# A hybrid layer in one launch: where the recurrence's first block of inputs is loaded, and where its batch statistics are put together

## The chip, the cores and the metric

The kernel runs on one core of one Trainium2 chip. The metric is the device time of one launch in microseconds (us), the median over several executions. A core has five engines that run their own instruction streams: TensorE (PE, matrix products), VectorE (DVE), ScalarE (ACT), GpSimd (POOL) and SyncE (SP). Transfers between the chip's memory and the on-chip memory (SBUF) are issued by SP here, except for those that add to what stands at their destination, which POOL issues. All of them are carried by the core's 16 DMA engines.

## The reference, cut to what matters

Everything is float32. An image is 64 x 64 cells with 128 features, and there are 16 of them. Layer 0 adds a grid recurrence (a two-dimensional LSTM) to its input. Layer 1 first adds a landmark attention over the 4096 tokens of each image, then the part that the change touches:

```
# t: 16 images x 4096 tokens x 128 features, after the attention
Wx   = einsum('bti,hi->bth', layernorm(t), W)
mean, var = over all 16*4096 tokens, for each of the 128 features
Wx   = (Wx - mean) * rsqrt(var + 1e-5) * gamma + beta
y_t  = sigmoid(Wx_t + y_{t-1} @ V.T)        # scan over the tokens of an image, y_{-1} = 0
out  = t + y
```

The normalisation needs `mean` and `var` of all tokens before the first sigmoid can be taken.

## The kernel before, in words

Five stages follow each other: group statistics of the input (to about 110 us), the grid LSTM (to about 1,430 us), the landmarks, the attention (up to 3,712 us) and the recurrence (to the end). The change touches the last two.

**The attention** (`attention`) walks over 128 groups of 512 tokens, eight (`Q`) to an image, in software-pipelined steps: `step(s)` for `s` from 0 to 144. In one step one group is projected (`new`, group s), one is weighed (`mid`, s-8), one is compared (`nxt`, s-15), one is attended (`cur`, s-16) and one is finished (`prev`, s-17). So the last sixteen steps project nothing new, and the very last finishes group 127. The order of the instructions on PE, DVE, ACT and POOL is the order in which the program is written (`tc.manual_schedule`); only SP's order is chosen by a scheduler. Values of an image, spread by heads, stand in `vs[b % 2]`, two buffers `at_vh0` and `at_vh1` of 16 KB per partition each; the even images use the first. Their last readers are the convolution over the tokens (`convolve`, line 1026, and `convolve_edges`, line 1038). For image 14 these are in steps 128 to 131.

Finishing a group means: `measure` (DVE, lines 1143 and 1144, then POOL, lines 30, 31, 1148 and 1149) and `normalise` (ACT, line 1154) make the layer norm, `turn_output` transposes it (PE, line 895), and `feed` multiplies it with W (PE, line 1161), takes the group's batch statistics into one entry of six numbers of `wx_stats` (DVE, line 1162), copies the product (ACT, line 1164) and stores it to `wx` in memory (SP, line 1165). `compare` makes DVE read four banks (line 1073, `topmost`). `output` makes `at_u`, the new t, on DVE (line 1135), and stores it to `t2` and `out` (SP, line 1137).

**The recurrence** (`recurrence`) doesn't scan 4096 tokens in order. An image is cut into 128 pieces of 32 tokens (`L = STEPS = 32`), which run side by side. Each piece begins 12 tokens (`WARM`) before its start to let the state converge, so a group of two images (`GI`) takes 12 + 32 = 44 rounds, plus one for a check whether the warm start agrees with the piece before. (If it doesn't, `in_order` does it again, token by token.) Eight such groups, `g` 0 to 7, run in four lanes: group g starts in round 0, 9, 18, 27, 45, 54, 63 and 72 (`starts`). The inputs of a group are loaded in two halves of 2.1 MB each, in four transfers a half: `w[1]` holds tokens 16 to 31 of each piece and is read in rounds 0 to 11 (the warm part) and 28 to 43 of the group, `w[0]` holds tokens 0 to 15 and is read in rounds 12 to 27. The tiles of the first kind have five buffers in turn, those of the second three. `due` says at which round a load stands in the program: `w[1]` ten rounds ahead of the group's start. A load whose buffer isn't free waits in SP's queue, and everything behind it waits too.

A round of one live group is a product with V (PE, line 1360), a scaled sum (DVE, line 1373) and a sigmoid (ACT, line 1381). The first round of a group has no product, and ACT reads the loaded input directly (line 1371), with the scale and shift that follow from the batch statistics (lines 1313 to 1317: DVE, POOL, DVE). Every second round of a group transposes two finished tokens (PE, line 1350) and copies them to `rc_tt` (ACT, line 1351, eight buffers); every fourth round POOL issues a transfer of 512 KB that adds `rc_tt` to `out` (line 1354). In a round the live groups follow each other on every engine in the order of their numbers, the copies come last.

The buffers of the loads, and their count, in the code before:

```
if n == 0:
    gr.w[h] = wp.tile([P, GI, G, HALF, C], F32, tag=f"w{h}", name=f"rc_w{h}", bufs=(3, 5)[h])
```

Of the kernel before, what the change touches and what calls it, by code (L numbers as in the profile page):

```python
# [8 lines left out]
F32 = mybir.dt.float32  # L9
AF = mybir.ActivationFunctionType  # L10
ALU = mybir.AluOpType
# [4 lines left out]
P = 128  # L16
# [3 lines left out]
HALF = STEPS // 2  # L20

AHEAD = 7
EPS = 1e-5


def inv_std(nc, pool, out, var, mhalf, tag):

    p, n = var.shape
    ve = pool.tile([P, n], F32, tag=f"{tag}_ve", name=f"{tag}_ve")
    nc.gpsimd.tensor_scalar(ve[:p], var, EPS, None, ALU.add)  # L30
    nc.gpsimd.tensor_tensor(out, ve[:p], mhalf[:p, :n], ALU.pow)


def group_stats(nc, tc, x, ident, mhalf, gmean, grstd, aside):
# [8 lines left out]
    with ExitStack() as ctx:  # L43
# [33 lines left out]
        def spread(v, copy):  # L77
# [3 lines left out]
            copy(ve, vg)  # L81
            nc.gpsimd.tensor_scalar(ve, ve, EPS, None, ALU.add)
            nc.gpsimd.tensor_tensor(grstd[:, v.cols], ve, mhalf[:, : v.n], ALU.pow)
# [61 lines left out]
def lstm_grid(nc, tc, x, fixed, stats, ident, mhalf, gmean, grstd, t1, acc):  # L145
# [17 lines left out]
    with ExitStack() as ctx:  # L163
# [110 lines left out]
        def factors(v):  # L274
# [4 lines left out]
            ve = sm.tile([P, 2, KT], F32, tag="ve", name="ls_ve")  # L279
            nc.gpsimd.tensor_scalar(ve[:, 0, :k], var, EPS, None, ALU.add)  # L280
            nc.gpsimd.tensor_scalar(ve[:, 1, :k], var, 1.0 + EPS, EPS * EPS, ALU.mult, ALU.add)
            nc.gpsimd.tensor_tensor(  # L282
# [145 lines left out]
def landmarks(nc, tc, acc, gamma, beta, wqkv, mask, ident, qm, km, pinvT):  # L428
# [12 lines left out]
    ITERS = 6  # L441
    GI = 8
    NT = NP * B // GI
    FLIP = range(NT * 3 // 8)
    W = GI // 2
    E = P // NP
# [348 lines left out]
    return a  # L795


def attention(nc, tc, t1, gamma, beta, wqkv, ident, mhalf, fixed, xp, rows, qm, km, pinvT, t2, wx, wx_stats, out):

# [5 lines left out]
    B, N, _ = t1.shape  # L807
    F = P
    M = km.shape[3]
    H = fixed[0].shape[1]  # L810
    DH = F // H
    K = N // P
    C = 4
    Q = K // C
    NP = H // 2
    E = W2 = 2 * DH
    GC = C * P
    BF = mybir.dt.bfloat16
    with ExitStack() as ctx:
        vp = ctx.enter_context(tc.tile_pool(name="at_v", bufs=1))  # L820
# [9 lines left out]
            return [bank(k, [P, GC]) for k in ks]  # L830

        bands, edges, wo, bo, wfT, ones, ones_b, minus, ident_b, heads, split, tops, avs = fixed
        vs = [vp.tile([P, H, K, DH], F32, name=f"at_vh{k}") for k in range(2)]
        R = vp.tile([P, K, H, DH], F32, name="at_R")

        low, high = slice(0, P // 2), slice(P // 2, P)
# [423 lines left out]
        with tc.manual_schedule(  # L1260
            engines={mybir.EngineType.PE, mybir.EngineType.DVE, mybir.EngineType.Activation, mybir.EngineType.Pool}
        ):
            projected(images[0])
            for g, a in enumerate(rows):
                group(g).xh = a
            turn_rows(group(0))
            for s in range(Q * (B + 2) + 1):
                step(s)


def recurrence(nc, tc, wx, wx_stats, t2, ffn_v, gamma, beta, ident, mhalf, out):

# [3 lines left out]
    B, H = wx.shape[:2]  # L1278
    N = t2.shape[1]
    L = STEPS  # L1280
    CH = N // L
    C = 16
    G = CH // C
    S = 4
    NB = L // S
    GI = 2
    LANES = 4
    PARTS = 8
    WARM = 12
    AGREE = 2.0 ** -18  # L1290
    NG = B // GI
# [2 lines left out]
    with ExitStack() as ctx:  # L1294
# [5 lines left out]
        with ExitStack() as fast:  # L1300
            wp = fast.enter_context(tc.tile_pool(name="rc_wp", bufs=1))
# [7 lines left out]
            vp = ps_t.tile([P, 4, P], F32, tag="t", name="rc_t")  # L1309
            nc.tensor.transpose(vp[:, 0, :], v, ident)  # L1310
            nc.vector.tensor_copy(vT, vp[:, 0, :])
            mv = cp.tile([P, 2], F32, name="rc_mv")
            nc.vector.bn_aggr(mv, wx_stats.rearrange("p c s -> p (c s)"))
            inv_std(nc, cp, scale, mv[:, 1:2], mhalf, "rc")
            nc.vector.tensor_mul(scale, scale, gamma)
            nc.vector.tensor_mul(shift, mv[:, 0:1], scale)
# [12 lines left out]

            def load(gr, n):  # L1330

                h, n = 1 - n // (PARTS // 2), n % (PARTS // 2)
                if n == 0:
                    gr.w[h] = wp.tile([P, GI, G, HALF, C], F32, tag=f"w{h}", name=f"rc_w{h}", bufs=(3, 5)[h])
                i, k = divmod(n, PARTS // 2 // GI)
                g = slice(k * G // 2, (k + 1) * G // 2)
                nc.sync.dma_start(
                    out=gr.w[h][:, i, g].rearrange("p g l c -> p (g l c)"),
                    in_=wx[gr.g * GI + i, :, h, g, :].rearrange("p g x -> p (g x)"),
                )  # L1340

            def turn(gr, s):

# [18 lines left out]
            def state(gr, n):  # L1362


                s = (n - WARM) % L
                w = gr.w[s // HALF][:, :, :, s % HALF, :]
                y = yp_.tile([P, GI, CH], F32, tag="y", name="rc_y", bufs=24)
                yg = y.rearrange("p i (g c) -> p i g c", c=C)
                gr.last = y
                if gr.z is None:  # L1370
                    nc.scalar.activation(yg, w, AF.Sigmoid, bias=shift, scale=scale)
                    return
                nc.vector.scalar_tensor_tensor(  # L1373
                    yg, w, scale, gr.z.rearrange("p i (g c) -> p i g c", c=C), ALU.mult, ALU.add
                )
                if n == WARM - 1:
                    gr.last = gr.y0 = yp_.tile([P, GI, CH], F32, tag="y0", name="rc_y0", bufs=LANES)
                    nc.vector.memset(gr.y0[:, :, 0:1], 0.0)
                    nc.scalar.activation(gr.y0[:, :, 1:CH], y[:, :, 0 : CH - 1], AF.Sigmoid, bias=shift)
                    return  # L1380
                nc.scalar.activation(y, y, AF.Sigmoid, bias=shift)  # L1381
                gr.ys[n - WARM] = y
# [10 lines left out]
            with tc.manual_schedule(  # L1393
                engines={mybir.EngineType.PE, mybir.EngineType.DVE, mybir.EngineType.Activation, mybir.EngineType.Pool}
            ):
                for t in range(max(starts) + ALL + 1):
# [10 lines left out]
                    for gr, n in live:  # L1407
                        s = n - WARM
# [75 lines left out]
@with_exitstack  # L1484
def kernel(ctx: ExitStack, tc: tile.TileContext, ins: dict, out: bass.AP):
    nc = tc.nc
    x = ins["x"]
    B, D0, D1, F = x.shape
    N = D0 * D1
    HEADS = ins["L1_attn_conv_w"].shape[0]  # L1490
    const = ctx.enter_context(tc.tile_pool(name="const", bufs=1))
    dram = ctx.enter_context(tc.tile_pool(name="scratch", bufs=1, space=DRAM))

    ident = const.tile([P, P], F32, name="ident")
    make_identity(nc, ident)
    mhalf = const.tile([P, 32], F32, name="mhalf")
    nc.gpsimd.memset(mhalf, -0.5)
    mask = head_mask(nc, const, HEADS)
    wqkv = const.tile([P, 3 * P], F32, name="wqkv")
    nc.scalar.dma_start(out=wqkv, in_=ins["L1_attn_w_qkv"])  # L1500
    gamma, beta, fgamma, fbeta = (
        column(nc, const, ins[f"L1_{k}"], k) for k in ("attn_gamma", "attn_beta", "ffn_gamma", "ffn_beta")
    )

    t1 = dram.tile([B, N, 2 * F + 4], F32, name="t1")
    t2 = dram.tile([B, N, F], F32, name="t2")
    wx = dram.tile([B, P, 2, N // 512, 256], F32, name="wx")
    pinvT = dram.tile([B, P, HEADS // 2 * D0], F32, name="pinvT")
    wx_stats = const.tile([P, B * N // 512, 6], F32, name="wx_stats")

    with tc.tile_pool(name="at_c", bufs=1) as ac, tc.tile_pool(name="at_x", bufs=1) as xp, tc.tile_pool(
        name="lmk", bufs=1
    ) as lmk:
        qm = lmk.tile([P, B, 2, D0], F32, name="qm")
        km = lmk.tile([P, B, 2, D0], F32, name="km")
        with tc.tile_pool(name="first", bufs=1) as first:
            acc = first.tile([P, 2, D0 * B // 2 // P, F], F32, name="acc")
            gmean = first.tile([P, B], F32, name="gmean")
            grstd = first.tile([P, B], F32, name="grstd")
            lw = [[ins[f"L0_conv_{k}{g}"] for g in GATES] for k in "wub"]  # L1520
            with tc.tile_pool(name="ls_c", bufs=1) as lc:
                start = ExitStack()
                cs = start.enter_context(tc.tile_pool(name="cb_s", bufs=1))
                cps = start.enter_context(tc.tile_pool(name="cb_ps", bufs=2, space=PSUM))
                fixed, jobs = attention_tiles(
                    nc, ac, cs, cps, dram, (N, F), ins["L1_attn_conv_w"], ins["L1_attn_w_out"],
                    ins["L1_attn_b_out"], ins["L1_ffn_W"], ident,
                )
                nc.vector.memset(acc, 0.0)
                lstm_fixed = lstm_tiles(nc, lc, (B, D0, F), *lw)  # L1530

                def stats(loads):
                    with start:
                        group_stats(nc, tc, x, ident, mhalf, gmean, grstd, jobs[:1] + loads + jobs[1:])

                lstm_grid(nc, tc, x, lstm_fixed, stats, ident, mhalf, gmean, grstd, t1, acc)
            rows = [load_rows(nc, xp, t1, 0, g) for g in range(3)]
            landmarks(nc, tc, acc, gamma, beta, wqkv, mask, ident, qm, km, pinvT)
        attention(
            nc, tc, t1, gamma, beta, wqkv, ident, mhalf, fixed, xp, rows, qm, km, pinvT, t2, wx, wx_stats,  # L1540
            out.rearrange("b i j f -> b (i j) f"),
        )
    recurrence(
        nc, tc, wx, wx_stats, t2, ins["L1_ffn_V"], fgamma, fbeta, ident, mhalf, out.rearrange("b i j f -> b (i j) f")
    )


# [19 lines left out]
```

## Time and profile before

| | |
|---|---|
| median of 3 runs | 4001.95 us (3993.2 to 4007.41) |
| the profiled execution, its own time | 4002.48 us |
| its span, first to last instruction | 4000.7 us |
| PE, DVE, POOL, ACT busy, share of the span | 94%, 77%, 71%, 63% |
| attention's last matrix product with W ends | 3711.9 us |
| first sigmoid of the recurrence starts | 3724.0 us |
| first sigmoid of groups 1, 2, 3 | 3745.5, 3764.0, 3780.8 us |
| first sigmoid of groups 4, 5, 6, 7 | 3823.1, 3847.1, 3874.3, 3895.3 us |
| last sigmoid | 3986.4 us |
| share of the DMA engines busy, 3,712 to 4,001 us | 97% |

The profile comes from one execution. Its page has the busy time of each engine, the span in 40 slices, the DMA queues, the chain of work that ended last, and groups of like instructions with the idle time ahead of them and what ended it. Closer views are answers to questions on the trace: the instructions in order of time ("start us, us, engine line op out<-in xcount [idle before <-releaser]"), the DMA traffic of a stretch, and the busy time of each engine in a stretch, with the clock that TensorE was granted (1.00 is full speed). Queue q1 carries what SP issues, queue q0 what POOL issues.

### The profile page before, as it was taken

The numbers are of one execution on the slowest core, as the hardware profiler recorded it, in microseconds if no ns is written. First come the engines' busy times: TensorE is split into PE (matmuls) and PEld (weight loads), VectorE is DVE, ScalarE is ACT, GpSimd is POOL, SyncE is SP. The second block draws the span as 40 slices with busy tenths as digits, with TensorE's granted clock in tenths as the row PEclk, the third lists the DMA queues.
The fourth block names the chain that finished last, engine by engine and source line by source line (L and its number), as shares of the span: only waits on it lengthen the run. The fifth ranks groups of instructions, "written<-read, shape, count | busy, mean of one in ns | idle before, by whom it ended". The sixth has DMA issues, their size and how long they took to land. (4 is left out here: it accounts for less than half of the span.)

```text
span 4000.7 us, 98082 instructions
## 1 busy us (share of the span) xinstructions
PE 3759.9 (94%) x36706; PEld 2534.3 (63%) x36706; DVE 3074.8 (77%) x7378; ACT 2510.8 (63%) x5131; POOL 2833.5 (71%) x4111
## 2 busy tenths in 40 slices
PE   6899999999999979789999999999999999988697
PEld 5667655555676669556666666666666666654486
DVE  8699999988898864338788788878887878757465
ACT  0466566566676644346777777777677777645597
POOL 0577877778888844158888888888888888876133
PEclk9899999999999979899999999999999999989798
DMA  9123332333332200113333333333333333223799
GB/s 339 59 73 81 82 83 81 84 83 86 87 87 79 72 26 5 45 26 85 89 92 87 95 89 88 95 84 96 85 92 95 83 95 85 82 65 91 243 267 175
DMA packets 500464, 383.75 MB, mean 96 GB/s; under 512 B 35976, under 2 KB 466960, under 8 KB 499984
## 3 DMA queue, kind: packets, MB, share of 16 engines
q1 hardware_dynamic: 477354, 340.74, 29.7%
q0 software_dynamic: 17728, 34.61, 4.8%
q8 instruction: 292, 4.78, 0.5%
q10 hardware_dynamic: 4902, 2.08, 0.2%
q14 instruction: 188, 1.54, 0.1%
HBM read 172.82 MB, written 204.48 MB: 94 GB/s over the span
## 5 line engine op out<-in xcount | busy, mean ns | idle before, releaser
L1018 POOL TENSOR_TENSOR at_total<-at_total,at_e 128x512 f32<-128x512 f32 x480 | 611.5, 1274 | 117.5 <-ACT at_e L991 86.2
L254 ACT ACTIVATE ls_g<-ls_z,ls_b 128x304 f32<-128x304 f32 (+26 forms) x950 | 496.3, 545 | 231.8 <-PE ls_z L252 197.4
L247 PE MATMUL ls_z<-ls_xn,ls_w 128*128 128x432 f32 (+28 forms) x1700 | 591.3, 495 | 3.9 <-POOL ls_xn L239 3.6
L247 PEld LDWEIGHTS ls_z<-ls_xn,ls_w 128*128 128x128 f32 x1700 | 312.8, 193 | 193.0 <-issue 98.4
L885 POOL TENSOR_SCALAR at_T<-at_T,at_nb 128x128 f32<-128x128 f32 x512 | 403.8, 797 | 13.3
L954 DVE TENSOR_REDUCE at_mxq<-at_bank 128x1 f32<-128x512 f32 x512 | 327.8, 683 | 83.4 <-PE at_bank L951 83.2
L252 PE MATMUL ls_z<-ls_hsum,ls_u 128*128 128x304 f32 (+26 forms) x1140 | 373.8, 465 | 0.0
L991 ACT ACTIVATE at_e<-at_bank 128x512 f32<-128x512 f32 x512 | 264.3, 603 | 116.3 <-PE at_bank L985 115.6
L1073 DVE TENSOR_REDUCE at_cmx<-at_bank 128x8 f32<-128x512 f32 x512 | 317.5, 683 | 18.2 <-PE at_bank L1066 12.5
L282 POOL TENSOR_TENSOR ls_tt<-ls_ve,mhalf 128x8 f32<-128x8 f32 (+2 forms) x190 | 314.2, 1654 | 15.8
L1102 ACT ACTIVATE at_eT<-at_bank 128x512 f32<-128x512 f32 x512 | 264.3, 603 | 75.0 <-PE at_bank L1099 74.8
L252 PEld LDWEIGHTS ls_z<-ls_hsum,ls_u 128*128 128x128 f32 x1140 | 215.9, 198 | 128.6 <-issue 78.0
L252 PE MATMUL ls_z<-ls_h,ls_u 128*128 128x304 f32 (+26 forms) x760 | 261.4, 468 | 27.1 <-DVE ls_h L369 27.1
L361 POOL TENSOR_TENSOR ls_g<-ls_g,ls_cell 128x304 f32<-128x304 f32 (+26 forms) x190 | 179.2, 943 | 127.5 <-ACT ls_g L254 111.3
L299 ACT ACTIVATE ls_tt<-ls_tt,ls_nb 128x128 f32<-128x128 f32 (+9 forms) x632 | 261.1, 479 | 4.3 <-POOL ls_nb L294 4.3
L365 ACT ACTIVATE ls_g<-ls_cell 128x304 f32<-128x304 f32 (+26 forms) x190 | 93.2, 491 | 263.3 <-DVE ls_cell L364 258.4
L239 POOL TENSOR_TENSOR ls_xn<-ls_xn,grstd 128x304 f32<-128x304 f32 (+26 forms) x190 | 202.8, 1068 | 51.1 <-DVE ls_xn L236 48.8
L1373 DVE SCALAR_TENSOR_TENSOR rc_y<-rc_w,rc_scale,rc_z 128x256 f32<-128x256 f32 x344 | 155.5, 480 | 107.1 <-PE rc_z L1360 105.4
L1360 PE MATMUL rc_z<-rc_y,rc_vT 128*128 128x256 f32 x688 | 186.1, 408 | 39.2 <-ACT rc_y L1381 28.4
L252 PEld LDWEIGHTS ls_z<-ls_h,ls_u 128*128 128x128 f32 x760 | 144.0, 198 | 120.8 <-issue 53.1
L1154 ACT ACTIVATE at_z<-at_u,at_nb,at_r 128x128 f32<-128x128 f32 x512 | 211.6, 505 | 11.9 <-POOL at_nb L1149 11.9
L1164 ACT COPY at_fx<-at_bank 128x512 f32<-128x512 f32 x128 | 133.0, 1039 | 126.2 <-DVE wx_stats L1162 103.5
(261 smaller groups left out, 9429.6 us busy)
## 6 DMA issues: line engine op xcount, KB each, us to landing
t<-ls_tt SPq DMA_DIRECT2D x392, 130.0 KB
at_T<-t SPq DMA_DIRECT2D x128, 264.0 KB
gs_xb<-in_x_dram SPq DMA_DIRECT2D x64, 512.0 KB
at_xh<-t SPq DMA_DIRECT2D x128, 256.0 KB
t<-at_u SPq DMA_DIRECT2D x128, 256.0 KB
out_dram<-at_u SPq DMA_DIRECT2D x128, 256.0 KB
wx<-at_fx SPq DMA_DIRECT2D x128, 256.0 KB
rc_w<-wx SPq DMA_DIRECT2D x64, 512.0 KB
```

What stands on the lines that cost most here:

```text
L247: nc.tensor.matmul(v.z[g][:, : v.total], wt[g], v.xn[:, : v.total], start=True, stop=True)
L252: nc.tensor.matmul(view(v, v.first.z[g]), ut[g], hin, start=False, stop=True, skip_group_check=True)
L254: nc.scalar.activation(a[:, : v.cols], z, AF.Tanh if g == 4 else AF.Sigmoid, bias=bt[g])
L282: nc.gpsimd.tensor_tensor(v.tt[:, 0:k, F + 2 : F + 4], ve[:, :, :k].rearrange("p r k -> p k r"), mhalf[:, : 2 * k].rearrange("p (k r) -> p ...
L299: nc.scalar.activation(v.tt[:q, k, F + 4 :], v.tt[:q, k, 0:F], AF.Identity, bias=v.nb[:q, k : k + 1], scale=v.tt[:q, k, F + 3 : F + 4],)
L885: nc.gpsimd.tensor_scalar(x[:, c, :], x[:, c, :], gr.nbt[:, 0, c : c + 1], gr.nbt[:, 1, c : c + 1], ALU.mult, ALU.subtract)
L954: nc.vector.tensor_reduce(gr.im.mxq[:, n : n + 1, gr.g], gr.s[n], AX.X, ALU.max)
L991: nc.scalar.activation(gr.e[:, n].rearrange("p c m -> p (c m)"), s[n], AF.Exp)
L1018: nc.gpsimd.tensor_tensor(total, total, e[:, :, c, :], ALU.add)
L1073: nc.vector.tensor_reduce(gr.mx[:, n].rearrange("p j c -> p c j"), gr.s[n].rearrange("p (c j m) -> p c j m", c=C, j=2), AX.X, ALU.max)
L1102: nc.scalar.activation(gr.eT[:, n], s[n], AF.Exp)
L1154: nc.scalar.activation(gr.z[:, c, :], gr.u[:, c, :], AF.Identity, bias=gr.nb[:, c : c + 1], scale=gr.r3[:, c : c + 1])
```

## The change

It does four things.

- A tile `spare` of 16 KB per partition is allocated for the whole kernel. In the attention it takes the place of `at_vh0`. In the recurrence it is the `w[1]` of group 0.
- The four loads of that half are issued in the attention, written after step 137 (`Q * (B + 1) + 1`), when nothing reads `spare` any more. SP's scheduler puts them between the other transfers of steps 128 to 131.
- After step 139 the function `sum_up` aggregates the first 120 of the 128 entries of `wx_stats` on DVE and writes the result, as one more entry of the same form, behind them. The recurrence then aggregates nine entries instead of 128.
- The ring of `w[1]` has four buffers instead of five. Groups 1 to 7 take them in turn. So group 5 gets the buffer of group 1, group 6 that of group 2, and group 7 that of group 3; before, group 5 got that of group 0, group 6 that of group 1, and group 7 that of group 2.

PE, ACT and POOL issue the same instructions in the same order; DVE has seven more (in `sum_up`), and SP as many transfers as before. In SP's order, `w[0]` of group 5 now stands ahead of its `w[1]`, and so it is for group 6.

```
+spare = const.tile([P, GI * N // 2], F32, name="spare")
...
-        vs = [vp.tile([P, H, K, DH], F32, name=f"at_vh{k}") for k in range(2)]
+        vs = [spare.rearrange("p (h k d) -> p h k d", h=H, k=K), vp.tile([P, H, K, DH], F32, name="at_vh1")]
...
             for s in range(Q * (B + 2) + 1):
                 step(s)
+                if s == Q * (B + 1) + 1:
+                    for n in range(PARTS // 2):
+                        load_part(nc, wx, spare, 0, n)
+                if s == Q * (B + 1) + 3:
+                    sum_up(nc, wx_stats, (B - 1) * Q, GC)
...
+def sum_up(nc, wx_stats, n, width):
+    end = wx_stats.shape[1]
+    mv, (even, odd) = wx_stats[:, end - 1, 1:3], (wx_stats[:, end - 2, k : k + 3] for k in (0, 3))
+    nc.vector.bn_aggr(mv, wx_stats[:, 0:n].rearrange("p c s -> p (c s)"))
+    for half in (even, odd):
+        nc.vector.memset(half[:, 0:1], n * width / 2)
+        nc.vector.tensor_copy(half[:, 1:2], mv[:, 0:1])
+        nc.vector.tensor_scalar(half[:, 2:3], mv[:, 1:2], n * width / 2, None, ALU.mult)
...
-            nc.vector.bn_aggr(mv, wx_stats.rearrange("p c s -> p (c s)"))
+            nc.vector.bn_aggr(mv, wx_stats[:, (B - 1) * N // 512 : B * N // 512 + 1].rearrange("p c s -> p (c s)"))
...
-                if n == 0:
-                    gr.w[h] = wp.tile([P, GI, G, HALF, C], F32, tag=f"w{h}", name=f"rc_w{h}", bufs=(3, 5)[h])
+                h = part_of(n)[0]
+                if n % (PARTS // 2) == 0:
+                    gr.w[h] = spare if (gr.g, h) == (0, 1) else wp.tile(
+                        [P, GI * G * HALF * C], F32, tag=f"w{h}", name=f"rc_w{h}", bufs=(3, 4)[h]
+                    )
+                if gr.w[h] is not spare:
+                    load_part(nc, wx, gr.w[h], gr.g, n)
```

`load_part` issues one of the four transfers of a half with the same shape as before.

More of the change, by code (lines that the diff above doesn't have):

```diff
@@ L23 @@
 EPS = 1e-5
+GI = 2
+PARTS = 8
 def inv_std(nc, pool, out, var, mhalf, tag):
@@ L795, in load_rows, with attention @@
     return a
-def attention(nc, tc, t1, gamma, beta, wqkv, ident, mhalf, fixed, xp, rows, qm, km, pinvT, t2, wx, wx_stats, out):
+def attention(nc, tc, t1, gamma, beta, wqkv, ident, mhalf, fixed, xp, rows, qm, km, pinvT, spare, t2, wx, wx_stats, out):
     B, N, _ = t1.shape
@@ L1268, in attention, with part_of, load_part, recurrence @@
                 step(s)
-def recurrence(nc, tc, wx, wx_stats, t2, ffn_v, gamma, beta, ident, mhalf, out):
+                if s == Q * (B + 1) + 1:
[11 more added lines that the diff above has]
+        nc.vector.tensor_scalar(half[:, 2:3], mv[:, 1:2], n * width / 2, None, ALU.mult)
+def part_of(n):
+    h, n = 1 - n // (PARTS // 2), n % (PARTS // 2)
+    i, k = divmod(n, PARTS // 2 // GI)
+    return h, i, slice(k * PARTS // 2, (k + 1) * PARTS // 2)
+def load_part(nc, wx, w, g, n):
+    h, i, part = part_of(n)
+    w = w.rearrange("p (i g x) -> p i g x", i=GI, g=PARTS)
+    nc.sync.dma_start(
+        out=w[:, i, part].rearrange("p g x -> p (g x)"), in_=wx[g * GI + i, :, h, part, :].rearrange("p g x -> p (g x)")
+    )
+def recurrence(nc, tc, wx, wx_stats, spare, t2, ffn_v, gamma, beta, ident, mhalf, out):
     B, H = wx.shape[:2]
@@ L1285, in recurrence @@
     NB = L // S
-    GI = 2
     LANES = 4
-    PARTS = 8
     WARM = 12
@@ L1330, in load @@
             def load(gr, n):
-                h, n = 1 - n // (PARTS // 2), n % (PARTS // 2)
-                if n == 0:
-                    gr.w[h] = wp.tile([P, GI, G, HALF, C], F32, tag=f"w{h}", name=f"rc_w{h}", bufs=(3, 5)[h])
[L1335 to L1340, printed above, removed]
+                h = part_of(n)[0]
+                if n % (PARTS // 2) == 0:
+                    gr.w[h] = spare if (gr.g, h) == (0, 1) else wp.tile(
+                        [P, GI * G * HALF * C], F32, tag=f"w{h}", name=f"rc_w{h}", bufs=(3, 4)[h]
+                    )
+                if gr.w[h] is not spare:
+                    load_part(nc, wx, gr.w[h], gr.g, n)
             def turn(gr, s):
@@ L1365, in state @@
                 s = (n - WARM) % L
-                w = gr.w[s // HALF][:, :, :, s % HALF, :]
+                w = gr.w[s // HALF].rearrange("p (i g l c) -> p i g l c", i=GI, g=G, c=C)[:, :, :, s % HALF, :]
                 y = yp_.tile([P, GI, CH], F32, tag="y", name="rc_y", bufs=24)
@@ L1508 @@
     pinvT = dram.tile([B, P, HEADS // 2 * D0], F32, name="pinvT")
-    wx_stats = const.tile([P, B * N // 512, 6], F32, name="wx_stats")
+    wx_stats = const.tile([P, B * N // 512 + 2, 6], F32, name="wx_stats")
+    spare = const.tile([P, GI * N // 2], F32, name="spare")
     with tc.tile_pool(name="at_c", bufs=1) as ac, tc.tile_pool(name="at_x", bufs=1) as xp, tc.tile_pool(
@@ L1539 @@
         attention(
-            nc, tc, t1, gamma, beta, wqkv, ident, mhalf, fixed, xp, rows, qm, km, pinvT, t2, wx, wx_stats,
+            nc, tc, t1, gamma, beta, wqkv, ident, mhalf, fixed, xp, rows, qm, km, pinvT, spare, t2, wx, wx_stats,
             out.rearrange("b i j f -> b (i j) f"),
@@ L1543 @@
     recurrence(
-        nc, tc, wx, wx_stats, t2, ins["L1_ffn_V"], fgamma, fbeta, ident, mhalf, out.rearrange("b i j f -> b (i j) f")
+        nc, tc, wx, wx_stats, spare, t2, ins["L1_ffn_V"], fgamma, fbeta, ident, mhalf, out.rearrange("b i j f -> b (i j) f")
     )
```

## The prediction

> **What bounds the kernel now.** The page's chain of work that ended last holds only the closing transfer, so I read the two places that the change touches in order of time: the seam between attention and recurrence, then the rounds in which the loads of groups 5, 6 and 7 fall.
>
> The seam, in order of time (start, duration, engine, line, operation):
>
> ```profile
> 3711.92 0.70 DVE L1162 BATCH_NORM_STATS2 wx_stats<-at_bank 128x6 f32<-128x512 f32 x1 [7.03 <-PE at_bank L1161]
> ...
> 3712.36 0.42 SPq L1337 DMA_DIRECT2D rc_w<-wx  x1
> 3712.65 3.62 DVE L1313 BATCH_NORM_AGGREGATE rc_mv<-wx_stats 128x2 f32<-128x768 f32 x1
> ...
> 3717.74 0.16 DVE L1317 TENSOR_TENSOR rc_shift<-ffn_beta,rc_shift 128x1 f32<-128x1 f32 x1
> ...
> 3722.72 1.28 ACT L1371 ACT_TABLE_LOAD   x1 [9.02 <-DMA rc_w<-wx]
> 3724.02 0.60 ACT L1371 ACTIVATE rc_y<-rc_w,rc_shift,rc_scale 128x256 f32<-128x256 f32 x1
> ```
>
> The statistics are ready at 3717.90, yet ACT waits for the first load until 3722.72. The load ends last here; the aggregation of 3.62 us is hidden behind it.
>
> In the attention's last steps DVE looks like this from one `at_u` to the next:
>
> ```profile
> 3664.07 0.69 DVE L1135 TENSOR_TENSOR at_u<-at_bank,at_T 128x512 f32<-128x512 f32 x1 [0.34 <-PE at_bank L1133]
> ...
> 3672.68 0.70 DVE L1162 BATCH_NORM_STATS2 wx_stats<-at_bank 128x6 f32<-128x512 f32 x1 [0.48 <-PE at_bank L1161]
> 3673.73 0.69 DVE L1135 TENSOR_TENSOR at_u<-at_bank,at_T 128x512 f32<-128x512 f32 x1 [0.34 <-POOL at_T L885]
> ```
>
> A step takes 9.66 us and DVE idles 0.82 us of it, in two waits that lie inside its own chain. DVE is the bound there.
>
> In the recurrence I looked at the DMA traffic from 3800 to 3812 us. SP issues the four loads of group 4's `w[0]` at 3800.06, and nothing else is loaded (queue, packets, MB, share of 16 engines):
>
> ```profile
> q0 software_dynamic: 615, 1.17, 55.1%
> q1 hardware_dynamic: 576, 2.10, 51.1%
> ```
>
> Together over 100%: the DMA engines are full, and the 2.10 MB share them about evenly with the stores. Narrower stretches put the last of it at 3811.7 us, so the half takes 11.6 us. From 3716 to 3756, with no stores, q1 moves 16.00 MB in 40 us, 0.40 MB/us, at which a half takes 5.2 us; from 3880 to 3892 the stores alone move 2.47 MB, 2.5 us for each of 512 KB.
>
> ACT where stores fall behind and where groups 5 and 7 start, then DVE in round 70, from the instructions in order of time:
>
> ```profile
> 3845.43 0.58 ACT L1351 COPY rc_tt<-rc_t 128x512 f32<-128x512 f32 x1 [2.73 <-DMA out_dram<-rc_tt]
> ...
> 3847.12 0.59 ACT L1371 ACTIVATE rc_y<-rc_w,rc_shift,rc_scale 128x256 f32<-128x256 f32 x1
> ...
> 3895.32 0.58 ACT L1371 ACTIVATE rc_y<-rc_w,rc_shift,rc_scale 128x256 f32<-128x256 f32 x1
> ```
> ```profile
> 3889.09 1.77 DVE L1373 SCALAR_TENSOR_TENSOR rc_y<-rc_w,rc_scale,rc_z 128x256 f32<-128x256 f32 x4 [0.83 <-PE rc_z L1360]
> ```
>
> Before group 5 ACT waits 2.73 us for a store to free a buffer, and 2.58 us once more at 3862.8. After each, TensorE's clock drops; the windows' fields are start:end, length, five engines' busy time, clock, DMA share, GB/s:
>
> ```profile
> 3846.00:3850.00 4.00, 3.53 (x12) 2.87 (x13) 1.92 (x4) 3.49 (x9) 1.21 (x1) 0.67 1.08 301
> ...
> 3870.00:3874.00 4.00, 3.62 (x11) 2.98 (x12) 1.55 (x4) 2.74 (x7) 2.41 (x2) 0.50 1.08 302
> ```
>
> A round free of such waits: rounds 27 to 45 last from 3780.84 to 3823.09, 42.25 / 18 = 2.35 us each. Rounds 45 to 72 last 72.23 us, where 27 x 2.35 = 63.4 would do: 8.9 us lost, 5.3 of it the two waits and 3.6 (1.8 each) the slow rounds after them.
>
> **What the Trainium skill says.** "DMA: Bandwidth & Descriptors", Queues, rings and completion order: each DMA engine takes turns between the queues that have work. The nearly equal shares above agree. The same page, Issuing engines are not separate DMA queues: transfers of all engines run on the same 16 and interleave, so a load can't pass the stores by coming from SP; the 55.1% and 51.1% agree. "TensorE: Matmul & The Clock Gate", What's actually happening: an idle window of about 3.4 us halves the clock. Here waits of 2.7 us are followed by a mean clock of 0.67, so I take longer waits to cost as much or more. "ScalarE: Activation LUTs", What ACT_TABLE_LOAD costs: 1283 ns; the trace has 1.28 us, after the wait.
>
> **The change part by part.** *The first load.* Four issues of 0.55 us on SP and 2.1 MB move to steps 128 to 131. On SP, the stores of `wx`, `t2` and `out` and the prefetches of `at_T` stand behind them; SP issues four transfers in a step of about 10 us or more, and the loads wait for PE's convolution of the same step. DMA is busy 33% from 3625 to 3712, so 5.2 us of traffic hides there: 0, up to 1 us if a prefetch is late.
>
> *The short aggregation.* Two rows give its price: 6 elements 0.18 us, 768 elements 3.62, so 4.5 ns an element. Nine entries are 54 elements: 0.40 us. From its end to the end of the shift the trace has 1.63 us (3716.27 to 3717.90). So the shift stands at 3712.65 + 0.40 + 1.63 = 3714.7, and after the table load (1.28 us, still behind the wait) the first sigmoid starts at about 3716.0 instead of 3724.0: -8.0 us. The statistics end last there now.
>
> *sum_up.* 720 elements: 3.4 us. Six operations on one column: 0.16 us each as at line 1317, 0.9 in all. Together 4.3 us, between `at_u` of step 139 and `measure` of step 140. Behind it on DVE stand `measure`, for which POOL, ACT and PE wait in turn, and the four reads of line 1073. DVE has no idle time outside its chain, and the steps after have none to win it back: +4.3 (at least 3.4, the aggregation alone; at most 4.6). The seam as a whole is worth -3.7.
>
> *Four buffers instead of five.* Group 5's `w[1]` now waits for the last read by group 1, in round 9 + 43 = 52, and is needed in round 54; before it waited for group 0, round 43. Group 6 waits for round 61 and starts in 63, group 7 for 70 and 72. Two rounds of lead instead of eleven, three times. The lead in us, from round 70: group 3 comes first on DVE, its sum ends at 3889.09 + 0.48 = 3889.57, and ACT comes to group 7's first sigmoid at 3895.32: 5.75 us. The load takes 11.6 us from issue, and then some time to release its reader. For the very first load that is 1.5 us (q1 has moved it by about 3721.2, ACT goes on at 3722.72); I take 1.4. So ACT waits 11.6 + 1.4 - 5.75 = 7.3 us, and all lanes with it, for ACT takes them in order: the next rounds' products and sums of the other groups wait for sigmoids behind it. Bounds: with the DMA engines to itself 5.2 + 1.1 to the first byte (3712.36 to 3713.4) + 1.4 = 7.7, a wait of 1.9; at the half share of the full stretch 3824 to 3860 (7.03 MB in 36 us, 10.8 for a half) behind 2.7 us of queued stores (issue 3800.06, first bytes about 3802.8) 14.9, a wait of 9.1. The clock costs 1.8 each (0 to 2.5). Together 3 x (7.3 + 1.8) = 27.3 us. During such a wait no store is issued and one to three leave, so the 8.9 us that stores cost before go: -8.9 (half of it in the worst case). Net +18.4.
>
> *Sum.* -3.7 + 18.4 = +14.7 us on the profiled execution's 4002.48 (span 4000.7 and 1.8 around it): 4017.2. That execution lies 0.5 us over the median, so 4016.7, say 4017.
>
> **The rivals.** *The stores make room* (not slower). DMA work isn't increased, and 2.1 MB leave the crowded stage's neighbourhood; if the stores have drained when rounds 52, 61 and 70 come, a load takes 7.7 us from issue to release, each wait is 1.9 us with no clock loss, and -3.7 - 8.9 + 5.7 = -6.9 gives 3995; with no wait at all 3990 or less. The point of decision: 3 x (w + 1.8) = 8.9 + 3.7, a wait w of 2.4, thus 8.2 us from issue to release. Against it: stores issued between 3802 and 3900 take 8 to 28 us to land, so at least three are always queued. *The aggregation is absorbed*, or loads and stores meet half-way: 4.3 less, 4012. Against it: DVE's 0.82 us. *The seam gains nothing* because the first sigmoid finds another wait (V's copy at line 1311 stands behind the shift on DVE, 0.3 us), or the stores' waits stay: +8 to +9, 4025. Against it: V lands by 3713.9.
>
> **How the numbers follow.** Forecast (4008 to 4027, around 4017): 0.68. Stores make room: 0.17. Absorbed: 0.08. Worse: 0.07. A measurement of this kernel can tell about 0.3%, 12 us, from no change, so the lines lie at 3990 and 4014. Of the forecast 0.54 lies above 4014; with 0.07 of the worse case, slower has 0.61. Faster by that much needs the rival with no wait at all: 0.05. The rest, 0.34, is within. The range from 4001 to 4027 leaves out most of the rival below and the upper half of the worse case, 2 in 10.
>
> **What would show it.** First sigmoid 3.4 us after the last statistics begin to aggregate, where it is 11.4 now; line 1313 at 0.4 us, its new copy in the attention at 3.4, and the attention's end 4.3 later; groups 5, 6 and 7 each behind an ACT wait of 5 to 9 us that ends with a DMA of `rc_w`; no wait on `out_dram<-rc_tt`; a clock of 0.5 to 0.7 after each. If a load is released within 8 us of its issue, I am wrong; so too if group 5's load is issued before round 52.

## The result, and the profile after

The changed kernel takes 4013.23 us (median of 11 runs, 4005.12 to 4021.91), the kernel before 3998.88 us in the same comparison (11 runs, 3984.65 to 4007.41). The ratio is 1.004, with a 95% interval of 1.0026 to 1.0054: slower by 14 us where 14.7 were forecast. The profiled execution has a span of 4017.6 us, 16.9 more than that of before.

The seam after the change, in order of time:

```profile
3714.14 0.70 DVE L1165 BATCH_NORM_STATS2 wx_stats<-at_bank 128x6 f32<-128x512 f32 x1 [7.03 <-PE at_bank L1164]
...
3714.87 0.40 DVE L1347 BATCH_NORM_AGGREGATE rc_mv<-wx_stats 128x2 f32<-128x54 f32 x1
...
3715.95 0.54 SPq L1168 DMA_DIRECT2D wx<-at_fx  x1
...
3716.74 0.16 DVE L1351 TENSOR_TENSOR rc_shift<-ffn_beta,rc_shift 128x1 f32<-128x1 f32 x1
...
3719.83 1.28 ACT L1404 ACT_TABLE_LOAD   x1 [3.90 <-DMA wx<-at_fx]
3721.13 0.60 ACT L1404 ACTIVATE rc_y<-spare,rc_shift,rc_scale 128x256 f32<-128x256 f32 x1
```

The aggregation takes 0.40 us, and the shift is ready 2.76 us after the last statistics begin, both as worked out (before, 5.98). But ACT doesn't go on then. It waits 2.9 us more, for the store of the last `at_fx` to memory. From the last statistics to the first sigmoid are 6.99 us, where 12.10 were before and 4.1 were forecast.

The new work in the attention, and what DVE then waits for:

```profile
3661.74 3.40 DVE L1284 BATCH_NORM_AGGREGATE wx_stats<-wx_stats 128x2 f32<-128x720 f32 x1
...
3665.44 0.28 DVE L1146 BATCH_NORM_STATS2 at_st<-at_u 128x6 f32<-128x128 f32 x1
...
3669.89 0.72 DVE L1115 STREAM_TRANSPOSE at_dT<-at_bank 128x512 f32<-128x512 f32 x1 [0.40 <-PE at_bank L1112]
...
3673.85 0.69 DVE L1130 TENSOR_TENSOR at_oT<-at_bank,at_oT 128x512 f32<-128x512 f32 x1 [1.31 <-PE at_bank L1129]
```

All of `sum_up` is 3.70 us from its start to the next statistics, for its six small operations overlap. Yet from the statistics of group 122 to those of group 124 pass 24.5 us instead of 19.3: +5.2. PE, which had waited 4.7 us for DVE, is slow in this step. The windows' fields are the same as ahead of the prediction, the clock last but two:

```profile
3665.70:3669.70 4.00, 1.86 (x12) 0.63 (x16) 3.65 (x12) 0.50 (x2) 1.84 (x5) 0.65 0.31 81
3669.70:3673.80 4.10, 4.10 (x25) 2.37 (x18) 2.47 (x4) 2.22 (x5) 3.77 (x10) 0.50 0.00 0
```

Groups 5, 6 and 7 in the recurrence, ACT in order of time:

```profile
3850.86 0.60 ACT L1404 ACTIVATE rc_y<-rc_w,rc_shift,rc_scale 128x256 f32<-128x256 f32 x1 [9.45 <-DMA rc_w<-wx]
3880.26 0.60 ACT L1404 ACTIVATE rc_y<-rc_w,rc_shift,rc_scale 128x256 f32<-128x256 f32 x1 [7.82 <-DMA rc_w<-wx]
3910.02 0.60 ACT L1404 ACTIVATE rc_y<-rc_w,rc_shift,rc_scale 128x256 f32<-128x256 f32 x1 [7.25 <-DMA rc_w<-wx]
```

All three wait for their load. SP issues these halves with the first four transfers of each of the following rows (the rows of 8 and 6 go on with another half):

```profile
3835.62 6.66 SPq L1302 DMA_DIRECT2D rc_w<-wx  x8
...
3866.43 1.93 SPq L1302 DMA_DIRECT2D rc_w<-wx  x4
...
3896.99 5.34 SPq L1302 DMA_DIRECT2D rc_w<-wx  x6
```

So the halves take 15.2, 13.8 and 13.0 us from issue to release; without its wait ACT would have come 5.8, 6.0 and 5.8 us after the issue. Together they wait 24.5 us, and this is all that ACT waits for DMA between 3800 and 4000 us: the waits on the stores of before are gone.

```profile
ACT rc_y L1404 <- DMA rc_w<-wx: 24.5, 3, 9.5
```

The rounds 45 to 72 (first sigmoid of group 4 to that of group 7) take 89.8 us instead of 72.2, and from there to the end of the last sigmoid are 94.0 instead of 91.6. The clock after each wait:

```profile
3850.90:3854.90 4.00, 3.39 (x11) 2.81 (x12) 0.90 (x2) 3.21 (x7) 1.49 (x2) 0.53 1.07 297
...
3880.30:3884.30 4.00, 3.24 (x7) 2.15 (x8) 0.96 (x2) 3.31 (x8) 1.20 (x1) 0.50 0.53 71
...
3910.00:3914.00 4.00, 3.33 (x10) 2.77 (x11) 0.84 (x2) 3.26 (x7) 0.22 (x1) 0.50 1.08 302
```

So the two profiled executions differ thus: sum_up +5.2, first sigmoid -5.1, rounds 45 to 72 +17.6, the rounds after +2.5, the end -0.3. That is +19.9. The other -3.0, which make it 16.9, lie in the attention, in the main in steps 129 to 132; of these more at the end.

### The profile page after: what moved, and what is told of

Read it like the earlier page. It is cut to its first block, busy times and chain, and to the rows that moved or that the text cites. A ratio compares the mean times of both kernels' runs of the same rounds, so it can differ in the third digit from the quotient of the medians.

```text
span 4017.6 us, 98088 instructions
## 1 busy us (share of the span) xinstructions
PE 3763.9 (94%) x36706; PEld 2537.4 (63%) x36706; DVE 3075.5 (77%) x7385; ACT 2511.4 (63%) x5131; POOL 2833.2 (71%) x4111
## 5 line engine op out<-in xcount | busy, mean ns | idle before, releaser
L1387 POOL DMA_DIRECT2D out_dram<-rc_tt x64 | 77.4, 1209 | 207.1 <-ACT rc_tt L1384 205.2
L1406 DVE SCALAR_TENSOR_TENSOR rc_y<-rc_w,rc_scale,rc_z 128x256 f32<-128x256 f32 x317 | 143.4, 480 | 92.4 <-PE rc_z L1393 89.4
```

## The experiments

The theory: the loss comes from the ring of four, which makes three loads wait for a buffer that comes free two rounds ahead of their reader, while stores fill the DMA engines. The seam is worth nothing, because `sum_up` costs in the attention what the earlier start brings. The rivals: the loads are late whatever buffer they get, because the DMA engines are full; or the aggregation is absorbed, and something else is slow.

Times are medians, each beside runs of the kernel before on the same chip. The ratio isn't simply the quotient of the two medians.

| kernel | us | before, us | ratio (95%) |
|---|---|---|---|
| changed | 4013.23 | 3998.88 | 1.004 (1.0026 to 1.0054) |
| e1_spare_again | 3998.92 | 4001.45 | 0.999 (0.9978 to 1.0002) |
| e2_no_sum_up | 3994.3 | 4001.45 | 0.9981 (0.997 to 0.9992) |
| e3_sum_up_only | 4006.6 | 4001.45 | 1.0013 (1.0002 to 1.0024) |
| e4_no_stores | 3984.32 (one run) | 4001.45 | |
| e5_all_three | 3984.62 | 4002.2 | 0.9951 (0.9937 to 0.9965) |
| e5b_all_three (the same kernel) | 3990.2 | 3997.72 | 0.998 (0.9965 to 0.9995) |
| e6_fx_room | 4016.42 | 4002.2 | 1.0026 (1.0009 to 1.0043) |
| e7_no_sum_up_fx_room | 3992.19 | 3997.72 | 0.9992 (0.9977 to 1.0006) |
| e8_spare_for_7 | 4015.3 | 4002.2 | 1.0033 (1.0022 to 1.0044) |

**The spare tile again for group 5**

```
-                    gr.w[h] = spare if (gr.g, h) == (0, 1) else wp.tile(
+                    gr.w[h] = spare if (gr.g, h) in ((0, 1), (5, 1)) else wp.tile(
...
-                if gr.w[h] is not spare:
+                if (gr.g, h) != (0, 1):
```

> The changed kernel, but group 5 takes the spare tile for its first half once group 0 has done with it, so that groups 5, 6 and 7 wait for groups 0, 1 and 2 again, as before the change. Late-load theory (the 17 us come from loads that wait for a buffer two rounds ahead of their reader): no wait of ACT on a load at groups 5, 6 and 7; between the first sigmoids of groups 4 to 7 some 24, 27 and 21 us as before instead of 30.7, 29.4 and 29.8; time within 3 us of the kernel before. Rival (the load is late because the DMA engines are full of stores, whatever buffer it goes to): waits of 7 us stay, and 14 us over the kernel before.

Between the first sigmoids of groups 4 to 7 are 25.2, 24.0 and 21.9 us, 71.0 together. No wait on a load is left; the waits on stores are back. ACT's waits for DMA in this kernel, 3800 to 4000 us:

```profile
ACT rc_tt L1384 <- DMA out_dram<-rc_tt: 5.9, 5, 2.8
```

One assignment of a buffer takes the whole loss away, with the same amount of traffic. The first rival falls: full DMA engines alone make no load late when its buffer comes free eleven rounds ahead. And the rest of the change, early load and early aggregation together, is worth nothing that can be told from zero.

**No aggregation in the attention**

```
-                if s == Q * (B + 1) + 3:
-                    sum_up(nc, wx_stats, (B - 1) * Q, GC)
...
-            nc.vector.bn_aggr(mv, wx_stats[:, (B - 1) * N // 512 : B * N // 512 + 1].rearrange("p c s -> p (c s)"))
+            nc.vector.bn_aggr(mv, wx_stats[:, 0 : B * N // 512].rearrange("p c s -> p (c s)"))
```

(on e1_spare_again)

> As e1_spare_again, and without the aggregation in the attention: the recurrence aggregates all 128 entries. Theory (DVE bounds the attention's last steps, and at the seam the whole aggregation hides behind the last store of at_fx, whose room the first state takes): the step of 14.7 us goes back to 9.7, the first sigmoid starts about 7.3 us after the last statistics begin (7.0 with the short aggregation, 12.1 before), so 5 us less than e1_spare_again and 4 to 5 us less than before. Rival (the short aggregation is what lets the recurrence start early): the first sigmoid 3.2 us later than with it, 2 us less than e1_spare_again at most.

The step that had `sum_up`, 13.75 us in e1_spare_again and 14.66 in the changed kernel, is back at 9.67, and the first sigmoid starts 7.43 us after the last statistics begin. So beside e1_spare_again (7.07 at the seam) the short aggregation saves 0.4 us there, and in the attention it costs 4.1. The median is 4.6 us under that of e1_spare_again; the two intervals overlap, so the size rests on the trace. With e1's ring this is faster than the kernel before, by 0.2%.

**sum_up alone, on the kernel before**

```
                 step(s)
+                if s == Q * (B + 1) + 3:
+                    sum_up(nc, wx_stats, (B - 1) * Q, GC)
```

(with the entries for its result, and the aggregation of nine entries in the recurrence)

> The kernel before with the aggregation in the attention alone: five buffers, no spare tile, the first load where it was. Theory: the attention ends 5 us later, the first sigmoid still waits for its load 12.1 us after the last statistics begin, so 5 us slower than before. Rival (the aggregation is absorbed by DVE's idle time): no change. A third way, that the early statistics help: 3 us faster, which needs the first load not to end last.

5.2 us slower in the medians, and the trace has the same +5.2 in the two steps; the seam takes 13.0 us, not less. So the aggregation isn't absorbed, and without the early load it brings nothing.

**No stores in the recurrence**

```
-                    nc.gpsimd.dma_start(out=rows, in_=gr.tt, accum_op=ALU.add)
+                    pass
```

> The changed kernel without the transfers that add the states to the output (the output then lacks them), so that the loads have the DMA engines to themselves. If sharing with the stores makes the loads long, ACT waits about 2 us at groups 5, 6 and 7 instead of 9.5, 7.8 and 7.3. If it is the transfer's own time and the two rounds of lead, 7 us stay.

ACT in order of time:

```profile
3833.58 0.60 ACT L1404 ACTIVATE rc_y<-rc_w,rc_shift,rc_scale 128x256 f32<-128x256 f32 x1 [1.92 <-DMA rc_w<-wx]
3856.90 0.60 ACT L1404 ACTIVATE rc_y<-rc_w,rc_shift,rc_scale 128x256 f32<-128x256 f32 x1 [3.27 <-DMA rc_w<-wx]
3882.35 0.60 ACT L1404 ACTIVATE rc_y<-rc_w,rc_shift,rc_scale 128x256 f32<-128x256 f32 x1 [3.00 <-DMA rc_w<-wx]
```

8.2 us in place of 24.5. SP issues the halves at 3825.87, 3847.62 and 3873.56, so they take 7.7, 9.3 and 8.8 us from issue to release. Both things are needed: two rounds are too few even for a load without the stores beside it, and the stores make up two thirds of the wait. The first, 1.92, is the lower bound of the prediction.

**The spare tile for group 7**

```
-                    gr.w[h] = spare if (gr.g, h) == (0, 1) else wp.tile(
+                    gr.w[h] = spare if (gr.g, h) in ((0, 1), (7, 1)) else wp.tile(
```

(and the load issued for group 7 as in e1_spare_again)

> The changed kernel, but the spare tile goes to group 7 instead of to nobody, so that groups 5 and 6 stay two rounds ahead only and group 7 has its load early. Late-load theory, counted: waits of 8 to 10 us at groups 5 and 6, none at group 7; one third of the loss goes, the time is about 6 us under the changed kernel and 9 to 11 us over the kernel before. Rival (the loss is a matter of the DMA engines' total work, which doesn't change): group 7's wait turns into waits on the stores of the same size, and the time stays at the changed kernel's.

The time can't be told from the changed kernel's. The trace shows why the third doesn't simply go. ACT in order of time, then its waits for DMA, 3800 to 4000 us:

```profile
3846.69 0.60 ACT L1404 ACTIVATE rc_y<-rc_w,rc_shift,rc_scale 128x256 f32<-128x256 f32 x1 [6.63 <-DMA rc_w<-wx]
3878.76 0.60 ACT L1404 ACTIVATE rc_y<-rc_w,rc_shift,rc_scale 128x256 f32<-128x256 f32 x1 [9.89 <-DMA rc_w<-wx]
3902.01 0.59 ACT L1404 ACTIVATE rc_y<-spare,rc_shift,rc_scale 128x256 f32<-128x256 f32 x1
```
```profile
ACT rc_y L1404 <- DMA rc_w<-wx: 16.5, 2, 9.9
...
ACT rc_tt L1384 <- DMA out_dram<-rc_tt: 3.6, 2, 2.7
```

Group 7 waits no more, as the theory says, and the rounds 63 to 72 take 23.3 us, 6.5 less than in the changed kernel. But rounds 45 to 63 take 3.5 us more: the wait at group 6 is longer, 9.9 us instead of 7.8, and 3.6 us of waits on stores come back. So rounds 45 to 72 take 86.8 us, only 3.0 under the changed kernel. The waits on stores end at 3833 and 3838 us, ahead of group 5 and long before the wait that was removed. SP issues group 7's load at 3809 us here, as soon as group 0 is done with the buffer, so its 2.1 MB run among the stores of that time; that they bring these waits back fits in time, but no run tests it alone. The expectation of 6 us was wrong in counting the waits as three equal and independent ones. The rival that it names is half right: not at group 7, but ahead of group 5, ACT waits for stores again. From group 7 to the end of the last sigmoid are 93.7 us, hardly less than with the wait (94.0); this stretch lies between 90.6 and 92.9 in the seven profiles without a wait on a load at groups 5 to 7, and why it is longer here stays open.

**Room of its own for at_fx**

```
-            fx = wk.tile([P, GC], F32, tag="fx", name="at_fx", bufs=1)
+            fx = fx_room
...
+    fx_room = const.tile([P, 512], F32, name="at_fx")
```

> The changed kernel with at_fx in room of its own alone. Theory: the first sigmoid starts 3.4 us after the last statistics begin instead of 7.0, the waits of 9.5, 7.8 and 7.3 us stay, so 3 to 4 us less than the changed kernel, some 12 us more than the kernel before. Rival (another wait at the seam): 7.0 us and the changed kernel's time.

The seam in order of time:

```profile
3714.01 0.70 DVE L1165 BATCH_NORM_STATS2 wx_stats<-at_bank 128x6 f32<-128x512 f32 x1 [7.03 <-PE at_bank L1164]
...
3715.82 0.54 SPq L1168 DMA_DIRECT2D wx<-at_fx  x1
...
3716.84 1.28 ACT L1404 ACT_TABLE_LOAD   x1 [1.04 <-DVE rc_shift L1351]
3718.13 0.60 ACT L1404 ACTIVATE rc_y<-spare,rc_shift,rc_scale 128x256 f32<-128x256 f32 x1
```

The first sigmoid starts 4.12 us after the last statistics begin; the wait on the store is gone and the shift ends last. (Where this expectation and the next say 3.4 I had counted from the aggregation, which begins 0.7 later.) The store held ACT up only because the first state is laid where `at_fx` stood: with the tile elsewhere, the same store still runs, and ACT doesn't wait for it. The waits at groups 5 to 7 stay, 21.7 us in all. The gain of 3 us can't be seen in the times; it rests on the trace.

**All three mended**

```
             if prev:
                 normalise(prev)
+            if s == Q * (B + 2):
+                sum_up(nc, wx_stats, (B - 1) * Q, GC)
...
-                if s == Q * (B + 1) + 3:
-                    sum_up(nc, wx_stats, (B - 1) * Q, GC)
```

(with the spare tile for group 5 and the room for `at_fx`)

> As e1_spare_again (group 5 takes the spare tile), with the aggregation moved into the last step, behind its normalise, where DVE waits 7.0 us for the last product, and with at_fx in room of its own that the recurrence doesn't take. Theory (the aggregation costs 5 us only where DVE has no idle time, and at the seam the first sigmoid waits for the store of at_fx because the first state takes its room): no step of 14.7 us in the attention, the first sigmoid 3.4 us after the last statistics begin instead of 7.1, so 5 + 3.7 us less than e1_spare_again and 8 to 9 us less than the kernel before (0.9978). Rival (the wait at the seam is another one that only ended with the store): 7 us stay at the seam, and 5 us less than the kernel before.

> The kernel of e5_all_three once more, on another occasion, because its time fell 8 to 9 us further than its profile's parts add up to (the profiled execution was 10 us under the kernel before). If the parts are all there is, 0.9975; if something else came with it, 0.995 again.

The seam of e5_all_three in order of time:

```profile
3703.37 3.37 DVE L1284 BATCH_NORM_AGGREGATE wx_stats<-wx_stats 128x2 f32<-128x720 f32 x1
...
3710.48 0.70 DVE L1165 BATCH_NORM_STATS2 wx_stats<-at_bank 128x6 f32<-128x512 f32 x1 [3.35 <-PE at_bank L1164]
3711.21 0.40 DVE L1347 BATCH_NORM_AGGREGATE rc_mv<-wx_stats 128x2 f32<-128x54 f32 x1
...
3713.31 1.28 ACT L1404 ACT_TABLE_LOAD   x1 [1.05 <-DVE rc_shift L1351]
3714.61 0.60 ACT L1404 ACTIVATE rc_y<-spare,rc_shift,rc_scale 128x256 f32<-128x256 f32 x1
```

The wait of DVE for the last product falls from 7.03 to 3.35 us: the aggregation has taken its place and delays nothing. Its steps are 9.67 us each, the seam 4.13 instead of 12.10. That is the whole 8 us which the change was after. The first occasion gave 0.9951, the second 0.998, which is what the parts add up to; what the first had beyond that isn't explained, and I count on 8 us.

**Without sum_up, with the room for at_fx** (the edits of e2_no_sum_up and e6_fx_room together)

> As e2_no_sum_up (spare tile again for group 5, all 128 entries aggregated in the recurrence), with at_fx in room of its own. Theory: the whole aggregation now ends last at the seam, 0.7 + 3.6 + 1.6 us and the table load of 1.3, so the first sigmoid starts 7.3 us after the last statistics begin, as in e2_no_sum_up, where the store hid it: the same time as that kernel, 0.998, and 3 us more than e5. Rival (the room of at_fx is worth something elsewhere too): as e5.

The seam takes 7.35 us, as expected: the whole aggregation ends last now (the shift is ready 0.07 us before ACT goes on, though the profile names a DMA of `rc_w` as the last). The median is 2.0 us over that of e5b_all_three beside it, in overlapping intervals. The interval includes 1, so that the small gain of e2_no_sum_up, which has the same seam, isn't confirmed by these runs.

## Why the prediction was right, point by point

- *The first load.* Forecast at no cost. e1_spare_again has it and is not slower than before. Where it is issued, from the statistics of group 111 to those of group 122, are 157.1 us in the kernel before, 157.0 to 157.3 in four profiles with the early load (e4, e5b, e6, e7) and 153.8 to 158.7 in the other five, where the steps differ as told at the end: no cost that can be told from this spread. Right.
- *The short aggregation.* 0.40 us forecast and measured, the shift at 2.76 as forecast. But the step "The statistics end last there now" failed: the store of `at_fx` ended last, and -8.0 became -5.1. I had looked for waits of the first sigmoid on what it reads, and not on what stands in the room that it writes. e6_fx_room shows it.
- *sum_up.* +4.3 forecast and at most 4.6, +5.2 measured. Its operations cost less (3.70), and PE at half its clock after the pause added the rest, about 1.5. In e1_spare_again PE pauses as long, but the low clock is shorter (see the end); the step is 13.75 us and the loss 4.1.
- *The seam as a whole.* -3.7 forecast, +0.1 measured; the rival that the seam gains nothing was right in this part, though not in the wait that it named (V's copy).
- *Four buffers.* The lead of 5.75 us was 5.8 to 6.0. The waits were 7.3, 7.3, 7.3 in the forecast and 9.45, 7.82, 7.25 in the trace, 24.5 against 21.9; the first load took 15.2 us, longer than the 13.0 assumed and a little past the upper bound of 14.9. The clock was forecast at 1.8 for each and cost 1.9 + 2.5 in all, 1.5 each: rounds 45 to 72 have 89.8 - 63.4 = 26.4 us over the undisturbed rounds, 24.5 of them waits, and 2.5 come after group 7 (DVE's sums of the third round behind its first sigmoid start after 7.1 us instead of 4.4). The 8.9 us of before are gone, as forecast. Net +20.1 for +18.4.
- *The sum.* +14.7 forecast, about +14 in the medians. Both parts were off the same way, the seam by 3.8 us and the ring by 1.7: they add up to +19.9 with the end, and this pair of executions had -3.0 from elsewhere. The mechanism of the ring and its place were right; the closeness of the sum is partly luck.
- *The rivals.* The stores didn't make room: the load needed 13 to 15 us, not 8.2.

In the terms of the Trainium skill, "DMA: Bandwidth & Descriptors", Queues, rings and completion order: engines take turns between queues with work. e4_no_stores agrees: take one queue's work away, and the other's transfer is released 5.4 us earlier on average (8.6 us after its issue instead of 14.0). It shows that the queues share the engines, not in what order they take turns.

## What to carry to other kernels

A buffer that is taken out of a ring is paid for by the loads that come round to it later, not by the one that moves: count for each load the time from the last reader of its buffer to its own reader, and set it against a transfer under the traffic of that moment. When a start is to come earlier, list what stands in the room that the first instruction writes, besides what it reads. And work for a bounding engine is free only in an idle gap of that engine; here one lay a few steps on, before the last product.

## What the runs showed of the hardware

A pause of 4.7 us on PE, behind DVE's new work, was followed by half the clock (0.50 from 3667 to 3673 us, 0.81 in the next 2 us), so that 3.7 us of work cost 5.2. The same pause isn't always followed by as much: in e1_spare_again the three windows of 2 us from 3671 to 3677 have 0.71, 0.50 and 0.93, and the cost is 4.1. What decides it no run here shows. And the same steps of the attention take different times between executions: in the kernel before, steps 129 and 130 take 17.0 us each, at a clock of 0.80; in the changed kernel's profiled execution they take 15.4 and 14.1, at 0.89 and 1.00, and so in that of e5_all_three (15.3 and 14.1), while e5b_all_three, the same kernel, has 17.0 twice. So a kernel can have either. Whether the early load makes the shorter steps more likely stays open: the two profiled kernels without it (before, e3_sum_up_only) both have 17.0. Such shifts are of the order of what a single wait is worth here, which is why the parts were compared within the profiles, and the times over many runs.
